# A one-core graph, scan and expert network: the lead-in of the scan stage, with the softplus of all channels ahead of step one

## The chip, the cores and the metric

The kernel runs on one core of one Trainium2 chip. A core has five instruction streams that run side by side and meet only at semaphores: TensorE (PE, matrix products into the PSUM memory), VectorE (DVE), ScalarE (ACT, functions of one tensor), GpSimd (POOL) and SyncE (SP, which here only issues transfers). Each stream takes its instructions strictly in order; an instruction that waits holds up everything behind it on the same engine. Transfers run on 16 DMA engines, whichever stream issued them. The metric is the device time of one execution in microseconds (us), lower is better.

## The reference

The input is `x` (4096 tokens of 256 features) and a sparse 4096 x 4096 matrix `adj`. Two layers follow each other, each a graph part and a mixture of experts. The change touches only the graph part of layer 0, a graph convolution with a Mamba block behind it:

```python
h = jax.nn.relu(adj @ x @ gcn_w + gcn_b)          # x already layer-normed
h = (h - mu) * lax.rsqrt(var + EPS) * ln_g + ln_b
xz = h @ w_in                                     # 256 -> 2 x 512 channels
xconv = sum(xpad[k:k + L] * conv_w[:, k] for k in range(4)) + conv_b
u = jax.nn.silu(xconv)
dbc = u @ w_xp                                    # 16 + 16 + 16 columns
dt = jax.nn.softplus(dbc[:, :16] @ w_dt + b_dt)   # 512 channels
dA = jnp.exp(dt[:, :, None] * A[None])            # 16 states per channel
dBu = dt[:, :, None] * B[:, None, :] * u[:, :, None]
hst = dAt * hst + dBut; y = hst @ Ct              # one token after the other
y = (y + u * D_skip) * jax.nn.silu(z) @ w_out
```

The scan over tokens is a recurrence for each of 512 x 16 pairs of channel and state. After it come the experts of layer 0 and the whole of layer 1, which the change leaves alone.

## The kernel before

**Chunks and steps.** The tokens are cut into 8 chunks of 512. For each chunk a *front* (class `Front`) prepares what the scan needs, and 32 *steps* (class `Step`) run the scan. The 512 channels are 4 blocks of 128 (`MB`), in two halves of two blocks (`H = 2`). A step covers 32 channels (a *group*, four to a block), four states on the partitions beside them and two states one after the other along the row, so 128 partitions by 1024 elements. A group is used in two steps: steps 0 to 3 are groups 0 to 3 with the first pair of states, steps 4 to 7 the same groups with the second pair.

**A step.** `inputs` (L1384, POOL) multiplies dt*u by B into `db`; `decays` (L1400, ACT, two instructions of 512) makes `da = exp(A*dt)`; `scan` (L1416, DVE) runs the recurrence over 1024 elements; `keep` (L1423, ACT) saves the last column in `state`; `product` (L1429, DVE) multiplies by C into `hc`, a ring of six buffers; `pair` (L1433) adds the two halves of `hc` by a transfer issued from POOL; `total` (L1441 and L1447, PE) sums groups into `psy`, two steps at a time and six steps late (`LAG = 6`); `gate` (L1455, DVE) finishes a block of channels.

**A front.** Its parts are methods named in two plans, `PLAN` and `EARLY`. In order: `do_gcn` (L949, PE), `do_biased` (L963, ACT), `do_stats` (L973, DVE), `do_normal` (L985, ACT), `do_turn` and `do_turned`, `do_xz` (L1016, PE), `do_conv` (L1033, PE), `do_silu` (L1043, ACT), `do_project` (L1053, PE), `do_scatter` (L1060, ACT, and a transfer to memory from which B and C are spread over partitions, L1126), `do_dt` (L1067, PE, one per block). Then softplus, written so that it keeps its accuracy, per half of the channels: `do_abs` takes the absolute value and the positive part (L1079, L1080, ACT, per block), `do_exp` (L1083, ACT) makes e = exp(-|v|), `do_plus` (L1086, L1087, ACT) makes (e + 1) - 1, `do_soft 0` (L1095, DVE) the rounding error of that, `do_log` (L1090, ACT) overwrites e with ln(1 + e), and `do_soft 1, 2, 3` (L1097, L1099, L1101, DVE) add up dt and make dt*u. `do_store` (L1108) writes both to memory, `dtd`, by two transfers from SP; `spread` (L1117) reads one group's 32 rows back from there with each row repeated on four partitions, into `dtu`, a ring of five buffers. ACT has a table of functions to load when it goes between exp, ln and silu; the loads are instructions of their own (ACT_TABLE_LOAD).

**The propagation** `adj @ x` of a later chunk (`propagation`, L877, PE) runs in *pieces* of two products among all this. A chunk has two halves of 32 pieces, 64 products. A product of 32-bit numbers is two passes on PE, and the rows of the profile count passes, so half a chunk is 128 of them. The adjacency comes in tiles `at` of 512 KB (L795, SP), three buffers, eight products to a tile. Both halves accumulate in one PSUM buffer `pt` (`ps_pt`, `bufs=1`); at the end of a half ACT copies it out into `pts` (L883), and the next half's first product waits for that copy. `advance(k)` emits k pieces, and where a half ends among them, the copy too.

**The order.** PE, DVE, ACT and POOL run in the order in which the program text emits instructions (a manual schedule); SP's order is set by a planner. The lead-in of chunk 0 runs the plans of its front with i from 4 to 26 and puts pieces of chunk 1's propagation behind single i by the table `FILL`:

```python
            prop, left = propagation(1), 2 * NT + 2 - late
            for i in range(4, 27):
                fr.at(i, Front.EARLY)
                fr.at(i)
                ...
                k = min(FILL.get(i, 0), left)
                advance(k)
                left -= k
            advance(left)
```

The first half of the channels passes softplus here (i = 20 to 25), its four groups are spread at i = 25, and the pieces that remain follow at i = 21, but for the last four, which fall into steps 0 to 2. The second half of the channels passes softplus inside steps 0 to 5 (L1596 puts i = 27 to 32 of front 0 into them). From step 3 on, the front of chunk 1 is worked on among the steps of chunk 0, and so on.

Of the kernel before, what the change touches and what calls it, by code (L numbers as in the profile page):

```python
# [10 lines left out]
F32 = mybir.dt.float32  # L11
BF16 = mybir.dt.bfloat16
I32 = mybir.dt.int32
AF = mybir.ActivationFunctionType
ALU = mybir.AluOpType
# [4 lines left out]
P = 128  # L20
CW = 512
# [25 lines left out]
def kernel(ctx: ExitStack, tc: tile.TileContext, out: bass.AP, **a):  # L47
    nc = tc.nc
# [6 lines left out]
    MB = DI // P  # L55
# [727 lines left out]
    with ExitStack() as s1:  # L783
        wp = s1.enter_context(tc.tile_pool(name="w_gnn0", bufs=1))
        w1p = s1.enter_context(tc.tile_pool(name="work1", bufs=1))
        w2p = s1.enter_context(tc.tile_pool(name="work2", bufs=2))
# [53 lines left out]
        H = MB // 2  # L840
        G4 = P // 32
# [4 lines left out]


        PE_RATIO = 1.0
        FILL = {6: 8, 7: 2, 9: 1, 12: 3, 14: 1, 17: 3, 18: 1, 19: 2, 20: 3, 21: 40}
        FILLED = {7: 1, 8: 2}  # L850
        PIECE, PE_STEP, DVE_STEP = 1.0, (1.8, 0.1), 4.25
        PE_COST = {"gcn": 2.5, "turn": 0.8, "xz": 2, "conv": 4, "project": 2, "dt": 1}
# [1 line left out]
        psts, fronts = {}, {}  # L854
# [44 lines left out]
        class Front:  # L899
# [24 lines left out]
            def __init__(self, c):  # L924
                self.c = c
                self.pts = psts.pop(c)
                self.dtd, self.dtu, self.bc = {}, {}, {}
                self.st = small.tile([P, TPC, 6], F32, name="ln_st")
                self.mv = small.tile([P, TPC, 2], F32, name="ln_mv")
                self.rs = small.tile([P, TPC], F32, name="ln_rs")  # L930
                self.nm = small.tile([P, TPC], F32, name="ln_nm")
                self.ps, self.psy = {}, {}
# [139 lines left out]
            def do_abs(self, m):  # L1072
                ps = self.ps.pop(("dt", m))
                b = m % H
                if b == 0:
                    self.sp = w1p.tile([P, 2, H, CW], F32, name="sp", tag="tmp")
                    self.t1 = w1p.tile([P, H, CW], F32, name="t1", tag="h")
                    self.dt, self.du = self.sp[:, 0], self.sp[:, 1]
                nc.scalar.activation(self.du[:, b, :], ps, AF.Abs, bias=b_dt[:, m:m + 1])  # L1079
                nc.scalar.activation(self.dt[:, b, :], ps, AF.Relu, bias=b_dt[:, m:m + 1])  # L1080

            def do_exp(self, a):
                nc.scalar.activation(self.du, self.du, AF.Exp, scale=-1.0)  # L1083

            def do_plus(self, a):
                nc.scalar.activation(self.t1, self.du, AF.Identity, bias=1.0)  # L1086
                nc.scalar.activation(self.t1, self.t1, AF.Identity, bias=minus1[:, :1])  # L1087

            def do_log(self, a):
                nc.scalar.activation(self.du, self.du, AF.Ln, bias=1.0)  # L1090

            def do_soft(self, a, i):
                t1, dt, du = self.t1, self.dt, self.du
                if i == 0:
                    nc.vector.tensor_tensor(t1, t1, du, ALU.subtract)  # L1095
                elif i == 1:
                    nc.vector.tensor_tensor(du, du, t1, ALU.subtract)  # L1097
                elif i == 2:
                    nc.vector.tensor_tensor(dt, dt, du, ALU.add)  # L1099
                else:  # L1100
                    nc.vector.tensor_tensor(  # L1101
                        du, dt, self.us[:, a * H:a * H + H, :], ALU.mult
                    )

            def do_store(self, a):
                self.dtd[a] = dram.tile([P, H, 2, CW], F32, name=f"dtd{self.c}_{a}")
                for k in range(2):
                    nc.sync.dma_start(self.dtd[a][:, :, k, :], self.sp[:, k])  # L1108
                fronts[self.c] = self

            def spread(self, g):

# [352 lines left out]
        with tc.manual_schedule(engines={  # L1465
# [13 lines left out]
            for _ in range(2 * NT + 2 - sum(FILLED.values())):  # L1479
                i = min(range(STEPS), key=lambda i: pe[i] - PE_RATIO * dve[i])  # L1480
# [4 lines left out]
            def advance(k=1, wait=False):  # L1485


                while k > 0:
                    k -= 1
                    if next(prop, None) and wait:  # L1490
                        break
                return k
# [50 lines left out]
            fr = Front(0)  # L1543
# [8 lines left out]
            for _ in range(EARLY_LISTS - NT // 4):  # L1552
                next(made)
            prop, left = propagation(1), 2 * NT + 2 - late
            for i in range(4, 27):
                fr.at(i, Front.EARLY)
                fr.at(i)
                if i == 6:
                    for _ in made:
                        pass  # L1560
                if i == 19:
                    for p in range(2):
                        fr.states("b", p)
                        fr.states("c", p)
                if i == 25:
                    for g in range(G4):
                        fr.spread(g)
                k = min(FILL.get(i, 0), left)
                advance(k)
                left -= k  # L1570
            advance(left)
            steps, tails, kept, gated, summed, owed = [], [], {}, [], 0, 0
            ALL = NC * STEPS
            for n in range(2):
# [4 lines left out]
            for n in range(ALL):  # L1579
                c, i = divmod(n, STEPS)  # L1580
                cur = steps[n]
                if i == 6 and c > 0:
                    if c < NC - 1:
                        kept[c - 1] = keep_gated(c - 1)
                    else:
                        tails.extend(Tail(c - 1, hh) for hh in range(2))
                if i == 8 and c == NC - 2:
                    tails.extend(
                        Tail(k, hh, kept[k], k < SLOW) for k in range(c) for hh in range(2)
                    )  # L1590
                if i == BEGIN:
                    fr = Front(c + 1) if c + 1 < NC else None
                    prop = propagation(c + 2) if c + 2 < NC else iter(())
                live = [(fronts[c], STEPS + i)] if n > 0 else []
                if c == 0 and i < 6:
                    live.insert(0, (fronts[0], 27 + i))  # L1596
                if i >= BEGIN and fr is not None:
                    live.append((fr, i))

                if n + 5 < ALL:  # L1600
                    c5, i5 = divmod(n + 5, STEPS)
                    if i5 % (2 * G4) < G4:
                        fronts[c5].spread(i5 // (2 * G4) * G4 + i5 % G4)
                if fr is not None:
                    if i == 27:
                        fr.states("b", 0)
                    elif i == 29:
                        fr.states("c", 0)
                    elif i == 30:
                        fr.states("b", 1)  # L1610
                if i == 1 and c > 0:
                    fronts[c].states("c", 1)

                cur.scan()
                cur.keep()
                if n + 1 < ALL:
                    steps[n + 1].join()
                if n + 2 < ALL:
                    steps.append(Step(n + 2))
                    steps[n + 2].decays()  # L1620
                for f, k in live:
                    f.at(k, Front.EARLY)
                if c == NC - 1 and i in NORMS:
                    NORMS[i]()
                if n > 0:
                    steps[n - 1].product()
                if n + 2 < ALL:
                    steps[n + 2].inputs()
                if n > 0:
                    steps[n - 1].pair()  # L1630
                for st in gated:
                    st.gate()
                gated = []
                if summed <= n - LAG or (summed <= n - 3 and not steps[summed].paired):
                    if steps[summed].total(steps[summed + 1]):
                        gated.append(steps[summed])
                    summed += 2
                for f, k in live:
                    f.at(k)
                for _ in range(TAILS.get((c, i), 1)):  # L1640
                    Tail.step(tails)
                if c == NC - 1:
                    for piece in NPIECES.get(i, ()):
                        piece()
                    if i == 24:
                        last = Last()
                        last.fetch()
                    elif i == 25:
                        last.first(0)
                    elif i == 27:  # L1650
                        last.residual(0)
                    elif i == 29:
                        for m in range(H, MB - 1):
                            last.add(0, m)
                owed = advance(pieces[i] + owed, True)
                if i == BEGIN - 1:
                    while owed:
                        owed = advance(owed, True)
# [613 lines left out]
```

## Time and profile before

| | us |
|---|---|
| median of 3 runs | 2342.67 |
| lowest and highest | 2336.9, 2344.26 |
| the profiled execution, its time | 2334.95 |
| its span, first to last instruction | 2333.1 |
| from the start to the first scan (L1416) | 171.94 |
| from the first scan to the start of the last | 1104.2 |
| from there to the end | 1057.0 |

The profiled execution lies 7.7 us under the median and 2.0 us under the lowest of the three runs; 1.85 us of its time lie outside the span. The profile is read by times from the start of the span. A row of the timeline gives the start, the duration, the engine, the line, the operation, what it writes and reads, the shape, how many instructions were merged (x), and in square brackets how long the engine stood idle before it and what ended that. PEld is the weight load of TensorE, SPq the time in which SP issues a transfer. The table by stretches gives each engine's busy time, TensorE's granted clock (1 is full), and the share of the DMA engines.

### The profile page before, as it was taken

Reading aid. Unit: us, or ns where it says so; the run is one execution under the profiler, and the core shown is the slowest. Engines: PE = TensorE matmul, PEld = TensorE weight load, DVE = VectorE, ACT = ScalarE, POOL = GpSimd, SP = SyncE. Lnnn points to the kernel's source line nnn. Section 1 sums busy time; section 2 is a strip of 40 time slices with the busy share of each in tenths; the row PEclk is TensorE's granted clock in tenths of the full one; section 3 lists DMA queues with packets and bytes.
Section 4 is the critical chain, followed back from the end, with each engine's and each line's share of the span. In section 5 each row is a group of like instructions: output and inputs, shape, how many; then the busy total and the mean of one; then the engine's idle time right before and its main releaser. Section 6 shows DMA issues by size and latency. Waiting matters only on the chain. (4 is left out here: it accounts for less than half of the span.)

```text
span 2333.1 us, 28789 instructions
## 1 busy us (share of the span) xinstructions
PE 2052.0 (88%) x8851; PEld 1451.2 (62%) x8851; DVE 1791.4 (77%) x2940; ACT 1308.2 (56%) x2386; POOL 1392.1 (60%) x1057
## 2 busy tenths in 40 slices
PE   7898989899998989988688699996899989899984
PEld 6665555555555564544355588784588778778773
DVE  4938999999999999998989699414438999954342
ACT  4136768677676867768686232322488778533221
POOL 1006777787777778776764354442057778856651
PEclk9899999999999999998788799998899999999997
DMA  7656897979889797887963799873355555477794
GB/s 240 212 168 177 203 286 170 273 180 247 220 199 281 168 273 183 241 226 193 259 190 122 228 346 354 280 225 114 118 178 173 179 160 180 142 237 221 251 307 150
DMA packets 299717, 498.77 MB, mean 214 GB/s; under 512 B 32459, under 2 KB 171711, under 8 KB 298656
## 3 DMA queue, kind: packets, MB, share of 16 engines
q1 hardware_dynamic: 241760, 383.28, 52.0%
q0 software_dynamic: 57792, 113.54, 21.5%
q8 instruction: 73, 1.20, 0.2%
q14 instruction: 92, 0.75, 0.1%
HBM read 384.01 MB, written 65.80 MB: 193 GB/s over the span
## 5 line engine op out<-in xcount | busy, mean ns | idle before, releaser
L1384 POOL TENSOR_TENSOR db<-dtu,bb 128x1024 f32<-128x1024 f32 x256 | 600.2, 2345 | 342.3 <-DVE hc L1429 177.4
L1416 DVE TENSOR_TENSOR_SCAN db<-da,state,db 128x1024 f32<-128x1024 f32 x256 | 599.1, 2340 | 44.5 <-ACT db L1409 29.8
L877 PE MATMUL pt<-at,gn 128*128 128x256 f32 x2048 | 487.7, 392 | 35.2 <-DMA at<-in_adjT_dram 18.1
L877 PEld LDWEIGHTS pt<-at,gn 128*128 128x128 f32 x2048 | 390.6, 195 | 144.2 <-issue 50.2
L1400 ACT ACTIVATE da<-dtu,negA 128x512 f32<-128x512 f32 (+1 forms) x512 | 350.2, 684 | 26.5 <-DMA dtu<-dtd 14.3
L1429 DVE TENSOR_TENSOR hc<-db,cb 128x1024 f32<-128x1024 f32 x256 | 341.5, 1334 | 15.3 <-PE psy L1447 15.2
L1962 PE MATMUL pf<-gn,f 128*128 128x256 f32 x1280 | 288.7, 386 | 0.0
L1962 PEld LDWEIGHTS pf<-gn,f 128*128 128x128 f32 x1280 | 246.9, 194 | 37.0 <-issue 3.3
L712 PE MATMUL ps_h<-xkT,wk 128*128 128x256 f32 x864 | 214.8, 390 | 15.8 <-DVE xkT L737 11.7
L697 PE MATMUL ps_y<-wk,hk 128*128 128x256 f32 x864 | 213.1, 382 | 0.2
L702 DVE TENSOR_TENSOR yk<-ps_y,bk 128x512 f32<-128x512 f32 x73 | 50.1, 686 | 205.7 <-PE ps_y L697 175.6
L1433 POOL DMA_DIRECT2D hc<-hc x232 | 201.8, 870 | 0.2
L712 PEld LDWEIGHTS ps_h<-xkT,wk 128*128 128x128 f32 x864 | 159.1, 193 | 54.2 <-DVE xkT L737 19.0
L1824 POOL DMA_INDIRECT x<-gnd,ls_idx x128 | 149.3, 1166 | 60.7 <-DMA gnd<-gn 21.3
L697 PEld LDWEIGHTS ps_y<-wk,hk 128*128 128x128 f32 x864 | 161.8, 191 | 21.9 <-ACT hk L716 1.4
L1423 ACT COPY state<-db 128x2 f32<-128x2 f32 x224 | 42.9, 191 | 218.5 <-DVE db L1416 218.3
L1016 PE MATMUL ps_xz<-hT,w_in 128*128 128x512 f32 x256 | 133.0, 669 | 33.1 <-ACT zs L1029 20.1
L1447 PE MATMUL psy<-hc,pick 128*32 128x256 f32 x1120 | 158.5, 411 | 0.0
L1824 POOL DMA_INDIRECT ring<-gnd,ls_idx x88 | 110.3, 1253 | 31.3 <-issue 11.9
L716 ACT ACTIVATE hk<-ps_h,d0r_b 128x256 f32<-128x256 f32 x104 | 49.1, 474 | 137.5 <-PE ps_h L712 132.3
L1447 PEld LDWEIGHTS psy<-hc,pick 128*32 128x32 f32 x1120 | 57.4, 116 | 106.7 <-issue 79.1
L1033 PE MATMUL ps_xz<-xc,dK 128*128 128x512 f32 x256 | 115.2, 598 | 0.0
(422 smaller groups left out, 3228.5 us busy)
## 6 DMA issues: line engine op xcount, KB each, us to landing
at<-in_adjT_dram SPq DMA_DIRECT2D x208, 512.0 KB, 4.4
dtu<-dtd SPq DMA_DIRECT2D x128, 512.0 KB, 5.8
hc<-hc POOLq DMA_DIRECT2D x232, 256.0 KB, 5.6
wk<-in_L_ffn_W_dram SPq DMA_DIRECT2D x70, 512.0 KB, 6.0
wk<-in_L_ffn_expert_w_dram SPq DMA_DIRECT2D x114, 256.0 KB, 4.0
dtd<-sp SPq DMA_DIRECT2D x32, 512.0 KB, 5.5
ls_at<-in_adj_dram SPq DMA_DIRECT2D x32, 512.0 KB, 8.0
hc<-in_adj_dram SPq DMA_DIRECT2D x16, 512.0 KB, 6.5
```

Of the source, the lines that this page charges most:

```text
L697: nc.tensor.matmul(ps[:, j, :], hT[:, m, j * P:(j + 1) * P], w[:, m, :], start=(m == 0), stop=(m == kb_out - 1),)
L712: nc.tensor.matmul(ps[:, j, :], w[:, d, m * P:(m + 1) * P], xT[:, d, :], start=(d == 0), stop=(d == DB - 1),)
L877: nc.tensor.matmul(pt[:, k, :], xl[:, j, k * P:(k + 1) * P], at[:, jj, :], start=(j == 0 and k == 0), stop=(j == NT - 1 and k == DB - 1),)
L1016: nc.tensor.matmul(ps, w_in[:, k, m * P:(m + 1) * P], self.hT[:, k, :], start=(k == 0), stop=(k == DB - 1),)
L1384: nc.gpsimd.tensor_tensor(self.db, self.dtu[:, 1:2, :].to_broadcast([P, 2, CW]), self.f.bc["b", self.p], ALU.mult,)
L1400: nc.scalar.activation(da[self.n % 2][:, j, j:], self.dtu[:, 0, j:], AF.Exp, scale=negA[:, q, m, s_:s_ + 1],)
L1416: nc.vector.tensor_tensor_scan(flat, da[self.n % 2].rearrange("p a t -> p (a t)"), flat, state[:, self.g, 2 * self.p:2 * self.p + 1], ALU. ...
L1429: nc.vector.tensor_tensor(self.hc, self.db, self.f.bc["c", self.p], ALU.mult)
L1433: nc.gpsimd.dma_start(self.hc[:, 0, :], self.hc[:, 1, :], accum_op=ALU.add)
L1447: nc.tensor.matmul(f.psy[r, t], pick, st.hc[:, j, t], start=False, stop=(self.p == 1 and j == last and w == 1),)
L1824: nc.gpsimd.indirect_dma_start(out=to[:, :], out_offset=None, in_=gnd[:, :], in_offset=bass.IndirectOffsetOnAxis(ap=lists.idx[:, q, s:s + ...
L1962: nc.tensor.matmul(pf[:, t, :], f[:, jj, t * P:(t + 1) * P], gn[:, j, :], start=(j == 0 and t % 2 == 0), stop=(j == NT - 1 and t % 2 == 1),)
```

## The change

In chunk 0 the softplus of all four blocks now stands in the lead-in, ahead of step 0, written out as calls in place of the plan. The second half of the channels gets `hc` buffers of its own for its three tensors. For chunk 0 `do_plus` is one DVE instruction in place of two on ACT. The first four groups' rows are no longer read back from memory: `straight` copies them on chip, from the 32 partitions of `dt` (k = 0) or dt*u (k = 1) to 128 partitions, by eight transfers issued from ACT's stream. The stores of chunk 0 to `dtd` (four transfers, used by the later groups) are issued from ACT as well, no longer from SP. Five pieces of the propagation stand ahead of `do_dt` of blocks 2 and 3 (two from i = 19, three by `FILL[20]`), and the others come after the second store, the last four in steps 0 to 2 as before. Steps 0 to 5 lose the calls for front 0's second softplus. What other chunks do is not changed.

```diff
-        FILL = {6: 8, 7: 2, 9: 1, 12: 3, 14: 1, 17: 3, 18: 1, 19: 2, 20: 3, 21: 40}
+        FILL = {6: 8, 7: 2, 9: 1, 12: 3, 14: 1, 17: 3, 18: 1, 19: 2, 20: 3}
...
             def do_abs(self, m):
                 ps = self.ps.pop(("dt", m))
                 b = m % H
-                if b == 0:
+                a = m // H
+                if b == 0 and self.c == 0 and a == 1:
+                    self.dt[a], self.du[a], self.t1[a] = (
+                        w2p.tile([P, 2, CW], F32, name="hc", bufs=6) for _ in range(3)
+                    )
+                elif b == 0:
                     self.sp = w1p.tile([P, 2, H, CW], F32, name="sp", tag="tmp")
...
             def do_plus(self, a):
-                nc.scalar.activation(self.t1, self.du, AF.Identity, bias=1.0)
-                nc.scalar.activation(self.t1, self.t1, AF.Identity, bias=minus1[:, :1])
+                t1, du = self.t1[a], self.du[a]
+                if self.c == 0:
+                    nc.vector.tensor_scalar(t1, du, 1.0, -1.0, ALU.add, ALU.add)
+                    return
+                nc.scalar.activation(t1, du, AF.Identity, bias=1.0)
+                nc.scalar.activation(t1, t1, AF.Identity, bias=minus1[:, :1])
...
             def do_store(self, a):
                 self.dtd[a] = dram.tile([P, H, 2, CW], F32, name=f"dtd{self.c}_{a}")
-                for k in range(2):
-                    nc.sync.dma_start(self.dtd[a][:, :, k, :], self.sp[:, k])
+                for k, t in enumerate((self.dt[a], self.du[a])):
+                    (nc.sync if self.c else nc.scalar).dma_start(self.dtd[a][:, :, k, :], t)
                 fronts[self.c] = self
+
+            def straight(self, k):
+
+                for g in range(G4):
+                    if k == 0:
+                        self.dtu[g] = w2p.tile([P, 2, CW], F32, name="dtu", bufs=5)
+                    rows = self.sp[32 * g:32 * g + 32, k, 0, :]
+                    nc.scalar.dma_start(
+                        self.dtu[g][:, k, :],
+                        bass.AP(rows.tensor, rows.offset, [rows.ap[0], (0, G4), *rows.ap[1:]]),
+                    )
...
-            for i in range(4, 27):
+            for i in range(4, 20):
...
-                if i == 25:
-                    for g in range(G4):
-                        fr.spread(g)
                 k = min(FILL.get(i, 0), left)
                 advance(k)
                 left -= k
-            advance(left)
+            for m in range(H):
+                fr.do_abs(m)
+            fr.do_exp(0)
+            fr.do_plus(0)
+            fr.do_soft(0, 0)
+            advance(FILL[20])
+            for m in range(H, MB):
+                fr.do_dt(m)
+            fr.do_abs(H)
+            fr.do_log(0)
+            for m in range(H + 1, MB):
+                fr.do_abs(m)
+            fr.do_exp(1)
+            for i in range(1, 4):
+                fr.do_soft(0, i)
+            for k in range(2):
+                fr.straight(k)
+            fr.do_store(0)
+            fr.do_plus(1)
+            fr.do_soft(1, 0)
+            fr.do_log(1)
+            for i in range(1, 4):
+                fr.do_soft(1, i)
+            fr.do_store(1)
+            advance(left - FILL[20])
...
-                if c == 0 and i < 6:
-                    live.insert(0, (fronts[0], 27 + i))
```

More of the change, by code (lines that the diff above doesn't have):

```diff
@@ L927, in __init__ @@
                 self.dtd, self.dtu, self.bc = {}, {}, {}
+                self.dt, self.du, self.t1 = {}, {}, {}
                 self.st = small.tile([P, TPC, 6], F32, name="ln_st")
@@ L1074, in do_abs @@
                 b = m % H
-                if b == 0:
+                a = m // H
[4 more added lines that the diff above has]
+                elif b == 0:
                     self.sp = w1p.tile([P, 2, H, CW], F32, name="sp", tag="tmp")
[L1077 to L1080, printed above, removed]
+                    self.t1[a] = w1p.tile([P, H, CW], F32, name="t1", tag="h")
+                    self.dt[a], self.du[a] = self.sp[:, 0], self.sp[:, 1]
+                nc.scalar.activation(self.du[a][:, b, :], ps, AF.Abs, bias=b_dt[:, m:m + 1])
+                nc.scalar.activation(self.dt[a][:, b, :], ps, AF.Relu, bias=b_dt[:, m:m + 1])
             def do_exp(self, a):
-                nc.scalar.activation(self.du, self.du, AF.Exp, scale=-1.0)
+                nc.scalar.activation(self.du[a], self.du[a], AF.Exp, scale=-1.0)
             def do_plus(self, a):
-                nc.scalar.activation(self.t1, self.du, AF.Identity, bias=1.0)
-                nc.scalar.activation(self.t1, self.t1, AF.Identity, bias=minus1[:, :1])
+                t1, du = self.t1[a], self.du[a]
[4 more added lines that the diff above has]
+                nc.scalar.activation(t1, t1, AF.Identity, bias=minus1[:, :1])
             def do_log(self, a):
-                nc.scalar.activation(self.du, self.du, AF.Ln, bias=1.0)
+                nc.scalar.activation(self.du[a], self.du[a], AF.Ln, bias=1.0)
             def do_soft(self, a, i):
-                t1, dt, du = self.t1, self.dt, self.du
+                t1, dt, du = self.t1[a], self.dt[a], self.du[a]
                 if i == 0:
```

## The prediction

> **What bounds the kernel now.** I read the table by stretches first, then the timeline of all engines over the lead-in, then VectorE's and TensorE's own timelines over the first steps. Row by row, the stretches are the lead-in, the first nine steps, the other steps, and all that follows the scan.
>
> ```profile
> 0.00:172.00 172.00, 145.83 (x558) 110.28 (x559) 102.54 (x321) 49.71 (x90) 13.34 (x26) 0.94 0.63 204
> 172.00:214.00 42.00, 34.71 (x115) 20.80 (x115) 34.98 (x30) 26.70 (x46) 26.21 (x16) 0.88 0.72 204
> 214.00:1276.00 1062.00, 948.53 (x3892) 569.88 (x3890) 995.91 (x666) 765.40 (x1567) 784.98 (x483) 0.94 0.83 218
> ```
>
> The third number after the length is VectorE: 995.91 of 1062 us (94%) from step 8 on, but 34.98 of 42 (83%) before. So a shift of VectorE at step 8 reaches the end of the kernel undiminished, and what can be gained lies ahead of 214. The lead-in, all engines:
>
> ```profile
> 143.50 8.90 PE L877 MATMUL pt<-at,gn 128*128 128x256 f32 x40
> ...
> 146.48 1.06 ACT L1083 ACTIVATE sp<-sp 128x1024 f32<-128x1024 f32 x1
> ...
> 152.43 0.59 ACT L883 COPY pts<-pt 128x512 f32<-128x512 f32 x1 [2.63 <-PE pt L877]
> 153.04 1.28 ACT L1090 ACT_TABLE_LOAD   x1
> ...
> 154.25 24.55 PE L877 MATMUL pt<-at,gn 128*128 128x256 f32 x112 [1.86 <-DMA at<-in_adjT_dram]
> ...
> 155.42 1.23 DVE L1097 TENSOR_TENSOR sp<-sp,t 128x1024 f32<-128x1024 f32 x1 [4.35 <-ACT sp L1090]
> ...
> 157.98 0.55 SPq L1108 DMA_DIRECT2D dtd<-sp  x1
> ...
> 171.94 2.35 DVE L1416 TENSOR_TENSOR_SCAN db<-da,state,db 128x1024 f32<-128x1024 f32 x1 [12.77 <-POOL db L1384]
> ...
> 186.73 0.57 ACT L883 COPY pts<-pt 128x512 f32<-128x512 f32 x1
> ...
> 186.85 1.22 DVE L1095 TENSOR_TENSOR t<-t,sp 128x1024 f32<-128x1024 f32 x1 [6.19 <-ACT t L1087]
> ```
>
> Two things are to be seen. VectorE waits 12.77 us for step 0 and 6.19 us in step 2, where the second softplus stands; that is the prize. And the two copies L883 sit tight behind PE: at 152.43 ACT waits for PE, and PE goes on at 154.25, delayed by a transfer alone. VectorE's steps (scans 4, 6, 8, and two products that waited for PE), then TensorE:
>
> ```profile
> 193.85 2.34 DVE L1416 TENSOR_TENSOR_SCAN db<-da,state,db 128x1024 f32<-128x1024 f32 x1
> ...
> 205.59 2.34 DVE L1416 TENSOR_TENSOR_SCAN db<-da,state,db 128x1024 f32<-128x1024 f32 x1
> ...
> 213.47 2.34 DVE L1416 TENSOR_TENSOR_SCAN db<-da,state,db 128x1024 f32<-128x1024 f32 x1
> ...
> 227.99 1.23 DVE L1429 TENSOR_TENSOR hc<-db,cb 128x1024 f32<-128x1024 f32 x1 [1.48 <-PE psy L1447]
> ...
> 236.05 1.23 DVE L1429 TENSOR_TENSOR hc<-db,cb 128x1024 f32<-128x1024 f32 x1 [0.99 <-PE psy L1447]
> ```
>
> ```profile
> 198.30 6.34 PE L1016 MATMUL ps_xz<-hT,w_in 128*128 128x512 f32 x8 [5.46 <-ACT h L963]
> ...
> 210.04 5.40 PE L1016 MATMUL ps_xz<-hT,w_in 128*128 128x512 f32 x8 [1.83 <-ACT zs L1029]
> ...
> 220.79 3.60 PE L1016 MATMUL ps_xz<-hT,w_in 128*128 128x512 f32 x8
> ```
>
> The same eight passes take 3.60 us in a busy stretch, 6.34 after 5.46 us idle, 5.40 after 1.83: a PE that stood still restarts at about half speed and loses 1.8 to 2.7 us.
>
> **The change part by part.** The built program of the changed kernel gives the order on each engine; times are from the rows.
>
> *Gone from the steps:* four VectorE sums (1.22 to 1.40 us), on ACT four absolute values and positive parts, the exp, two additions, the ln and a table load, and the 6.19 us that VectorE waited. *Gone from SP:* four stores and four reads at about 0.55 us each; nothing waits for SP's time here, so that saves nothing.
>
> *Softplus in one piece.* ACT is as before up to the end of the first exp, 147.54. PE does ten products more (20 passes x 8.90/40 = 4.45 us, to 147.95), then the two products for blocks 2 and 3 (1.98, to 149.9), then the ten that end the first half: 154.4, where it was 152.4. On ACT: absolute value and positive part of block 2 at 149.1 (as before, 1.16 us after their product began) to 150.35; table load and ln to 152.7; block 3 to 154.0; table load and exp to 156.4. The addition moved to VectorE is not shown in this form; the bounds are 0.77 (an L870 row, half the output bytes) and 1.23 us (L1097). I take 1.23; either ends, with `do_soft 0`, by 150.0, before ACT gets to the ln, so it costs nothing; if ACT came sooner, up to 1.2. VectorE's sums follow the ln at 1.26 apart: dt at 155.3, dt*u at 156.5.
>
> *Ten transfers in ACT's stream* (eight copies, two stores) stand from 155.3 between ACT and the second ln. ACT issues none in the trace of before. Low bound: nothing for issuing, but the built program makes the eighth copy wait for the first to land and the stores for the second copy and for an adjacency tile asked for at 154.4; with 4.4 us for a tile (median of the `at` loads) the second ln starts at 159 to 159.5. High bound: 0.87 us each, as POOL issues (L1433), to 164. I take SP's pitch in the B and C reads (142.88, 143.46, 144.10, 144.74: 0.6 each), the nearest row as it issues the same kind: 155.3 + 6.0 = 161.4. Then table load and ln 2.35, three sums 3.75, the second store 0.6, the copy L883 0.6: **the first copy ends at 168.7** (166.5 to 171.5). It stood at 153.0.
>
> *The wait that this adds.* The second half of the propagation needs that copy, since there is one `pt`. PE, with nothing else in its order, stands from 154.4 to 168.7. Behind it: 128 passes x 24.55/112 = 28.1 us, plus 2.5 for the restart (between the two rows above): 199.3. *On ACT*, the second copy stands behind the decays of step 3 and ahead of those of step 4; ACT waits there with everything queued behind until 199.9. It ended at 187.3 before. The SP queue's read of group 4 waits for the first store and holds back the adjacency loads behind it to about 167, but their buffers are only free at 172, so that is hidden by PE's stall (without it: up to 6 us).
>
> *Step 0* is not earlier either: its decays follow the first copy and a table load of 1.3: scan at 171.4 against 171.94. Its rows, copied by about 163, and POOL's 2.35 us are hidden; the on-chip copying gains 0.5.
>
> *Steps 4 to 8.* Decays of step 4 end at 201.5, scan at 201.6 against 193.85: +7.7. VectorE idles from about 185. Then the missing softplus pays: 3.6 us to scan 5 (4.70 before), 5.8 to scan 6 (7.04), the same 7.9 to scan 8: 218.9 against 213.47, **+5.4**.
>
> *PE catches up a little.* From 199.3: the graph products 6.6, eight passes 1.75, the z products warm 3.5 where 6.2 followed idling, eight passes 1.75: the first total starts at 213.0 (206.21). The next z products wait for ACT until 215.6 (210.04) after a shorter idle; warm, they end 3.8 later than before, cold 5.4. VectorE's two waits for PE (1.48, 0.99) shrink accordingly, so the shift that remains lies between 3.8 and 5.4: **+4.6 us**. Against the profiled execution's own 2334.95 that is 2339.6; on the median of the runs, 2342.67, it is **2347**. Each us of the first copy is a us of the result: break-even at 164.1.
>
> [...]
>
> **The rivals.** *Faster: the copies do not hold PE.* If PE's second half ran as early as now, scans would run from 171.4 at 3.57 us a step with 2.3 for the statistics of chunk 1: scan 8 at 202.3 in place of 213.47, 11 us gained, 2331. The idle 6.19 speaks for it; against it, the copy comes in ACT's order behind a store that needs the last sum. It decides if the first copy ends by 157.
>
> *Slower: transfers cost ACT more than SP.* At 0.87 to 1.1 us each (the first L1433 rows: 0.87 to 1.13), the first copy ends at 171.4 to 173.9, the sum is +7.3 to +9.8; landings as slow as those of `dtu` (5.8) add up to 1: 2350 to 2354. It decides from 0.84 us per transfer (first copy at 171.1). The wide, repeated read from 32 partitions, which no row shows, speaks for it; SP's even 0.6 speaks against.
>
> *Nothing to measure: cheap issue.* At the low bound the copy ends at 166.5 and the sum is +2.4; with PE's clock at 1.0 instead of 0.88 between 172 and 214 after its rest, another 3 us go: 2342.
>
> **How the numbers follow.** Differences under 0.3% (7.0 us) can't be told from no change here: the three runs spread over 7.4. Forecast 0.40, cheap issue 0.12, dear issue 0.33, faster 0.15. The forecast's own spread (first copy by 2 us, restart by 1, the measurement by 3) leaves a quarter of it above +7, the rest within; the cheap case is within, the dear one all but 0.03 above, the faster one all but 0.02 below. Slower 0.40, same 0.47, faster 0.13. The range drops the faster case and the outermost of the dear one: 2336 to 2356; the forecast alone is 2342 to 2352.
>
> **What would show it.** Right: PE idle some 14 us before L877's second half, released by ACT's copy; the second copy near 200; scan 0 within 1 us of 172; scan 4 near 201; scan 8 near 219; no more 6.19. Wrong: ACT spending well under or over 6 us on the ten transfers, first copy outside 166 to 172, or VectorE's rhythm after step 8 other than now.

## The result, and the profile after

The changed kernel takes 2345.95 us (median of 20 runs, 2338.96 to 2350.98) beside 2338.34 us for the kernel before (20 runs, 2328.79 to 2344.26). The ratio is 1.0035, with a 95% interval of 1.0021 to 1.0048: slower, by 7.6 us between the medians. Its profiled execution is the slowest of the 20, with a time of 2350.98 us and a span of 2349.1. One execution of a run below (transfers from SP) took 2484.97 us at a granted clock of 0.81; it is left out of that run's time and ratio.

The stretches of the profile after, cut as before (lead-in, first nine steps, other steps); columns are busy time of PE, PEld, DVE, ACT, POOL, then PE's clock, the DMA share and GB/s:

```profile
0.00:172.00 172.00, 129.49 (x480) 94.99 (x480) 107.06 (x324) 51.34 (x92) 17.92 (x28) 0.90 0.63 200
172.00:214.00 42.00, 37.55 (x153) 30.53 (x154) 20.49 (x13) 12.90 (x24) 10.69 (x7) 0.87 0.57 167
214.00:1276.00 1062.00, 948.27 (x3881) 568.73 (x3881) 998.78 (x675) 767.45 (x1571) 791.30 (x489) 0.94 0.84 219
```

From 214 on VectorE is as busy as it was (998.78 against 995.91). The loss is in the two rows above: PE does 16 us less in the lead-in, and VectorE 14 us less in the first steps. ScalarE's timeline says why (ACTq is the time in which ACT's sequencer issues transfers):

```profile
154.78 1.06 ACT L1089 ACTIVATE hc<-hc 128x1024 f32<-128x1024 f32 x1
154.86 9.20 ACTq L1127 DMA_DIRECT2D dtu<-sp  x8
164.10 3.39 ACTq L1118 DMA_DIRECT2D dtd<-sp  x2
167.57 1.28 ACT L1100 ACT_TABLE_LOAD   x1 [11.74 <-DMA dtu<-sp]
168.87 1.06 ACT L1100 ACTIVATE hc<-hc 128x1024 f32<-128x1024 f32 x1
173.99 1.78 ACTq L1118 DMA_DIRECT2D dtd<-hc  x2
175.81 0.58 ACT L883 COPY pts<-pt 128x512 f32<-128x512 f32 x1 [5.88 <-DVE hc L1111]
...
207.40 0.58 ACT L883 COPY pts<-pt 128x512 f32<-128x512 f32 x1 [22.04 <-PE pt L877]
```

Eight copies and two stores hold ACT's stream for 12.7 us (154.86 to 167.57). Their rows stand end to end, so ACT waits for nothing between them. The second ln is behind them, the sums behind the ln, the second pair of stores behind the sums, and the copy L883 behind all that. VectorE and TensorE:

```profile
169.96 2.74 DVE L1107 TENSOR_TENSOR hc<-hc 128x1024 f32<-128x1024 f32 x1 [12.01 <-ACT hc L1100]
172.73 1.23 DVE L1109 TENSOR_TENSOR hc<-hc 128x1024 f32<-128x1024 f32 x1
173.99 1.23 DVE L1111 TENSOR_TENSOR hc<-hc,us 128x1024 f32<-128x1024 f32 x1
179.23 4.59 DVE L1437 TENSOR_TENSOR_SCAN db<-da,state,db 128x1024 f32<-128x1024 f32 x2 [4.01 <-ACT da L1421]
...
209.50 2.35 DVE L1437 TENSOR_TENSOR_SCAN db<-da,state,db 128x1024 f32<-128x1024 f32 x1 [17.43 <-ACT state L1444]
...
226.49 2.34 DVE L1437 TENSOR_TENSOR_SCAN db<-da,state,db 128x1024 f32<-128x1024 f32 x1
...
247.44 1.22 DVE L1450 TENSOR_TENSOR hc<-db,cb 128x1024 f32<-128x1024 f32 x1 [0.74 <-PE psy L1468]
```

```profile
149.43 4.58 PE L877 MATMUL pt<-at,gn 128*128 128x256 f32 x20
176.45 30.92 PE L877 MATMUL pt<-at,gn 128*128 128x256 f32 x128 [22.44 <-ACT pts L883]
...
215.67 3.60 PE L1017 MATMUL ps_xz<-hT,w_in 128*128 128x512 f32 x8
...
223.05 3.70 PE L1017 MATMUL ps_xz<-hT,w_in 128*128 128x512 f32 x8 [0.21 <-ACT zs L1030]
```

PE stands for 22.44 us until ACT's copy, and then does the whole second half in one piece. VectorE's waits of 12.77 us ahead of step 0 and 6.19 for the second softplus are gone; in their place stand 12.01 us ahead of the second sums, 4.01 ahead of step 0 and 17.43 ahead of step 4, and scan 8 starts at 226.49, 13.0 us later. The z products (L1017) now run almost without a gap in 3.60 and 3.70 us, where they took 6.34 and 5.40. One line of the page's table of groups sums it up for the whole kernel: the propagation's largest wait is now for that copy, 28.8 us, where it was 18.1 us for the adjacency's tiles. Before, then after:

```profile
L877 PE MATMUL pt<-at,gn 128*128 128x256 f32 x2048 | 487.7, 392 | 35.2 <-DMA at<-in_adjT_dram 18.1
L877 PE MATMUL pt<-at,gn 128*128 128x256 f32 x2048 | 492.4, 395 | 49.8 <-ACT pts L883 28.8
```

### The profile page after: what moved, and what is told of

The parts are those of the page before. It is cut to its first block, busy times and chain, and to the rows that moved or that the text cites. A ratio compares the mean times of both kernels' runs of the same rounds, so it can differ in the third digit from the quotient of the medians.

```text
span 2349.1 us, 28799 instructions
## 1 busy us (share of the span) xinstructions
PE 2053.9 (87%) x8851; PEld 1456.0 (62%) x8851; DVE 1793.6 (76%) x2942; ACT 1303.8 (56%) x2382; POOL 1392.9 (59%) x1057
## 5 line engine op out<-in xcount | busy, mean ns | idle before, releaser
L877 PE MATMUL pt<-at,gn 128*128 128x256 f32 x2048 | 492.4, 395 | 49.8 <-ACT pts L883 28.8
L1421 ACT ACTIVATE da<-dtu,negA 128x512 f32<-128x512 f32 (+1 forms) x512 | 350.0, 684 | 12.1 <-DVE db L1437 3.6
L1017 PE MATMUL ps_xz<-hT,w_in 128*128 128x512 f32 x256 | 129.3, 653 | 26.7 <-ACT zs L1030 18.1
L1864 POOL DMA_INDIRECT ring<-gnd,ls_idx x88 | 110.3, 1253 | 31.3 <-DVE x L1880 12.7
```

Of the source, the lines that this page charges most:

```text
L877: nc.tensor.matmul(pt[:, k, :], xl[:, j, k * P:(k + 1) * P], at[:, jj, :], start=(j == 0 and k == 0), stop=(j == NT - 1 and k == DB - 1),)
L1017: nc.tensor.matmul(ps, w_in[:, k, m * P:(m + 1) * P], self.hT[:, k, :], start=(k == 0), stop=(k == DB - 1),)
L1421: nc.scalar.activation(da[self.n % 2][:, j, j:], self.dtu[:, 0, j:], AF.Exp, scale=negA[:, q, m, s_:s_ + 1],)
L1864: nc.gpsimd.indirect_dma_start(out=to[:, :], out_offset=None, in_=gnd[:, :], in_offset=bass.IndirectOffsetOnAxis(ap=lists.idx[:, q, s:s + ...
```

## The experiments

**The theory.** The copy L883 is late because it stands in ACT's order behind ten transfers, the second softplus and two stores; PE waits for it, and step 4 waits for PE. **Its rivals:** the softplus of all channels ahead of step 0 costs time by itself; the on-chip copies hold something else up; or ACT is simply a slow issuer. The first runs move one thing each; the last two also move the copy and some pieces of the propagation. Times in the table are from their profiles, in us. A ratio is to the kernel before as measured beside that run: 2338.34 us for the first result, 2336.24 (29 runs) for the changed kernel again, the copy early and the transfers from SP, 2338.83 (23 runs) for the last three. The "marker" is the start of the first scan behind the scan stage (L295), so it tells what reaches the end of the stage; from it to the end of the span the runs take 1048 to 1055 us, but for the one marked in the last column.

| run | first copy ends | scan 0 | second copy ends | scan 4 | scan 8 | marker | ratio (95%) |
|---|---|---|---|---|---|---|---|
| before | 153.0 | 171.9 | 187.3 | 193.9 | 213.5 | 1284.7 | |
| before, again | 151.8 | 171.8 | 188.5 | 195.1 | 214.7 | 1285.5 | |
| after | 176.4 | 179.2 | 208.0 | 209.5 | 226.5 | 1294.2 | 1.0035 (1.0021 to 1.0048) |
| after, again | 175.9 | 178.8 | 205.9 | 207.4 | 224.4 | 1294.1 | 1.0042 (1.0026 to 1.0059) |
| copy early | 156.1 | 177.9 | 190.4 | 191.9 | 208.9 | 1282.9 | 0.9979 (0.9963 to 0.9996) |
| transfers from SP | 160.3 | 165.9 | 197.9 | 199.4 | 216.4 | 1286.6 | 1.0008 (0.9991 to 1.0024) |
| plain rows | 171.4 | 174.2 | 202.4 | 203.9 | 220.9 | 1290.0 | 1.0197 (1.0173 to 1.0220), marked |
| copies from POOL | 155.1 | 172.3 | 193.3 | 194.8 | 211.8 | 1285.6 | 0.9985 (0.9971 to 1.0000) |
| rows from memory | 155.9 | 168.9 | 190.0 | 191.5 | 208.5 | 1280.0 | 0.9965 (0.9951 to 0.9980) |

### The two kernels again

No edit to either; the changed kernel and the kernel before, each profiled a second time.

> The changed kernel once more, to see how far its lead-in moves from one execution to the next. Theory: what sets the loss is the end of the first copy out of the accumulator (176.4 us in the first profile), because the product engine waits for it; if so it ends within 2 us of 176.4 again, TensorE stands idle 20 to 24 us ahead of the second half, scan 8 starts within 2 us of 226.5, and the ratio to the kernel before is 1.003 to 1.005. Rival (the copy's place was an accident of one execution, and the loss lies elsewhere): the copy ends below 172 and the ratio stays above 1.003.

> The kernel before once more, for its profile. If executions differ in the stages behind the scan and not in the scan, the first scan starts within 1 us of 171.9, scan 8 within 1 us of 213.5, the last scan within 3 us of 1276.1, and what differs in the span lies behind it.

The changed kernel took 2344.76 us, ratio 1.0042; the kernel before, in one execution, 2335.58. ACT's ten transfers take 12.1 us (12.7 the first time), PE's wait is 22.11 us, the marker is 8.6 us behind that of the kernel before (9.6 in the first pair). In the first profile after, the part behind the marker was 6.5 us longer than before (1054.9 against 1048.4); here both have 1048.3. So those 6.5 us belong to that execution and not to the change. Scan 8 came 2.1 us earlier than in the first profile of the changed kernel, and 1.2 us later than in the first of the kernel before: each just outside what was expected.

### The copy early

Five pieces that end the first half, and its copy L883, are emitted right behind the second exp, ahead of the transfers. Nothing else moves in the program text.

```diff
             fr.do_exp(1)
+            advance(6)
             for i in range(1, 4):
                 fr.do_soft(0, i)
...
-            advance(left - FILL[20])
+            advance(left - FILL[20] - 6)
```

> Only the first copy moves: the last five pieces of the half and the copy are emitted behind the second exp, ahead of the ten transfers of ACT. Theory (the copy's place in ACT's order is the loss): TensorE is idle under 3 us ahead of the second half, the second copy ends at 184 to 187, scan 0 stays at 177 to 180 because the second ln still stands behind the transfers, scan 4 at 190 to 194, scan 8 at 208 to 211 against 213.5 before and 226.5 changed; ratio to before 0.997 to 1.000. Rival (the transfers' traffic, or the bunched softplus itself, costs the time): scan 8 at 215 or later and a ratio of 1.002 or more.

It took 2330.89 us: faster than both kernels (2336.24 for the kernel before beside it). ACT's order, then PE's:

```profile
154.60 1.30 ACTq L1127 DMA_DIRECT2D dtu<-sp  x2
155.49 0.57 ACT L883 COPY pts<-pt 128x512 f32<-128x512 f32 x1
155.94 8.31 ACTq L1127 DMA_DIRECT2D dtu<-sp  x6
164.29 2.88 ACTq L1118 DMA_DIRECT2D dtd<-sp  x2
167.25 1.28 ACT L1100 ACT_TABLE_LOAD   x1 [11.20 <-DMA dtu<-sp]
...
189.78 0.59 ACT L883 COPY pts<-pt 128x512 f32<-128x512 f32 x1 [5.78 <-PE pt L877]
```

```profile
156.10 16.01 PE L877 MATMUL pt<-at,gn 128*128 128x256 f32 x64 [2.35 <-ACT pts L883]
173.04 7.17 PE L877 MATMUL pt<-at,gn 128*128 128x256 f32 x32 [0.92 <-DMA at<-in_adjT_dram]
182.57 7.17 PE L877 MATMUL pt<-at,gn 128*128 128x256 f32 x32 [2.36 <-DMA at<-in_adjT_dram]
```

The transfers are as dear as ever and the second ln starts at 167.25, as late as in the changed kernel; scan 0 stays at 177.9. Yet the whole loss is gone, and 1.8 to 2.6 us at the marker more than that, because PE waits 2.35 us and not 22.44. So the long transfers cause the loss through the copy that stands behind them; scan 0, which they make 6 us later than before, does not set step 4. That the early softplus or the transfers' traffic is the loss is ruled out. The second copy ends 3 us later than expected (190.4), since PE still waits 0.92 and 2.36 us for tiles.

### All transfers from SP

The eight copies and the four stores go to SP's stream; the order on ACT stays otherwise.

```diff
-                    (nc.sync if self.c else nc.scalar).dma_start(self.dtd[a][:, :, k, :], t)
+                    nc.sync.dma_start(self.dtd[a][:, :, k, :], t)
...
-                    nc.scalar.dma_start(
+                    nc.sync.dma_start(
                         self.dtu[g][:, k, :],
```

> Only the issuer changes: all twelve transfers of chunk 0's lead-in go from ACT's stream to SP's; the copy stays behind the second store in the program. Theory: ACT is then held by VectorE's sums alone, the second ln ends near 159 to 160, the first copy at 162 to 166, TensorE is idle 8 to 12 us, the second copy ends at 193 to 197, scan 8 at 212 to 217; ratio 0.999 to 1.002. If ACT's own issuing is slow, SP's twelve rows are all 0.5 to 0.7 us; if it is the backlog of the DMA engines, SP too has rows of 2 us among the copies. Rival (the copy's place does not matter): ratio as the changed kernel's, 1.003 or more.

It took 2338.31 us, no difference from the kernel before (2336.24). The second ln's table load starts at 157.45 and the first copy ends at 160.3, earlier than the 162 to 166 expected, so ACT is free; PE waits 6.89 us for the copy, less than the 8 to 12 expected. But SP needs as long for the same transfers as ACT did. SP's timeline, and PE's:

```profile
154.32 8.84 SPq L1127 DMA_DIRECT2D dtu<-sp  x8
163.25 2.34 SPq L1118 DMA_DIRECT2D dtd<-sp  x2
165.71 2.62 SPq L1118 DMA_DIRECT2D dtd<-hc  x2
168.41 3.26 SPq L795 DMA_DIRECT2D at<-in_adjT_dram  x3
```

```profile
160.33 9.14 PE L877 MATMUL pt<-at,gn 128*128 128x256 f32 x32 [6.89 <-ACT pts L883]
174.69 22.60 PE L877 MATMUL pt<-at,gn 128*128 128x256 f32 x96 [5.22 <-DMA at<-in_adjT_dram]
```

ACT is no slow issuer: 8.84 us on SP, 9.20 on ACT. The queue moves the loss instead of removing it: the adjacency's tiles now stand behind the transfers on SP, and PE waits 5.22 us for one. So the second copy ends at 197.9, just past the 193 to 197 expected.

### Plain rows

The eight copies read all 128 partitions once, in place of the 32 partitions of a group with every row repeated (four times; the expectation's "sixteen" is a slip). Bytes written and number of transfers stay. The first four groups of chunk 0 so get wrong rows of dt and dt*u; the expectation's "second chunk" is a slip too.

```diff
-                    rows = self.sp[32 * g:32 * g + 32, k, 0, :]
+                    rows = self.sp[:, k, 0, :]
...
-                        bass.AP(rows.tensor, rows.offset, [rows.ap[0], (0, G4), *rows.ap[1:]]),
+                        rows,
```

> Part changed: the eight straight copies read 128 partitions once instead of each group's rows repeated sixteen times, so the first four groups of the second chunk get the wrong rows of dt*u; bytes written and number of transfers stay. If the repeated read from few partitions makes the long rows (copies of about 2 us among copies of 0.6), the eight copies take about 5 us instead of 9.2, the second ln starts near 162 instead of 167.6, the first copy ends near 170 and the ratio falls to about 1.001. If the backlog of the queues makes them (the adjacency's tiles in flight and the copies' own bytes), the rows, the second ln (166 to 168), the first copy (175 to 176) and the ratio (1.004) stay.

The lead-in answers the question. ACT's timeline:

```profile
153.67 5.75 ACTq L1127 DMA_DIRECT2D dtu<-sp  x8
159.46 1.36 ACTq L1118 DMA_DIRECT2D dtd<-sp  x2
160.91 1.28 ACT L1100 ACT_TABLE_LOAD   x1 [6.26 <-DMA dtu<-sp]
```

The ten transfers take 7.2 us where they took 12.7. Of the three sums behind the second ln, two now run beside POOL's products (2.38 and 3.25 us, then 1.23 alone; 6.9 in all), so the first copy ends at 171.4 and not at 170. The instructions of L1127 one by one (minimum, median and maximum in ns), first of the changed kernel and then of this run:

```profile
L1127 ACTq DMA_DIRECT2D dtu<-sp x8: 561/857/2273, 154.9 to 163.3; - x8
...
DMA to landing us min/median/max: 4.9/4.9/5.6
```

```profile
L1127 ACTq DMA_DIRECT2D dtu<-sp x8: 533/627/869, 153.7 to 158.7; - x8
...
DMA to landing us min/median/max: 3.7/3.7/3.8
```

And the stretch of the copies, in the changed kernel and in this run:

```profile
156.20:164.00 7.80, 0.00 (x0) 0.00 (x0) 1.72 (x2) 0.00 (x0) 0.00 (x0) 0.66 0.90 238
```

```profile
154.50:159.50 5.00, 0.00 (x0) 0.00 (x0) 2.23 (x3) 0.14 (x1) 0.00 (x0) 0.65 1.03 381
```

The DMA engines are taken up in both (share 0.90 and 1.03), but the stretch with the repeated read moves 238 GB/s and the one with the plain read 381, the adjacency's tiles in flight included. So it is the way the rows are read, and not the number or the bytes of the transfers, that makes single issues up to 2.27 us long there and 0.87 at most here; how a slow read holds its issuer was not shown. The run changes two things at once, the number of partitions read (32 to 128) and the repetition of rows (every row four times, or once); which of them counts, no run here separates. The expectation that the rows would stay long whatever is read is disproved.

The time of the whole run, 2384.7 us, where a ratio of 1.001 was expected, must not be read as a price: the marker is 4.3 us earlier than in the changed kernel, and all that is lost lies behind it (1087.3 us in place of 1054.9). The wrong rows change what reaches the experts, and with it the amount of work; the weight loads of one line of the experts, after and here:

```profile
L712 PEld LDWEIGHTS ps_h<-xkT,wk x864: 185/190/365, 1327.3 to 2312.8; 128*128 128x128 f32 x173
```

```profile
L712 PEld LDWEIGHTS ps_h<-xkT,wk x928: 185/190/338, 1323.0 to 2341.2; 128*128 128x128 f32 x186
```

### Copies from POOL

The copy early (with one piece of the second half), the eight on-chip copies issued by POOL, the four stores by SP, emitted behind the softplus (SP, whose order is planned, still starts the first pair at 153.7); eight more pieces stand behind the last sum.

```diff
-                    (nc.sync if self.c else nc.scalar).dma_start(self.dtd[a][:, :, k, :], t)
+                    nc.sync.dma_start(self.dtd[a][:, :, k, :], t)
...
-                    nc.scalar.dma_start(
+                    nc.gpsimd.dma_start(
...
             fr.do_exp(1)
+            advance(7)
...
-            fr.do_store(0)
...
+            advance(8)
+            fr.do_store(0)
             fr.do_store(1)
-            advance(left - FILL[20])
+            advance(left - FILL[20] - 15)
```

> Straight copies issued by GpSimd, both stores by SyncE behind the softplus, the propagation's first copy on ScalarE ahead of the second ln. If ScalarE's order is the whole loss: the second ln near 157.5, the first copy ends near 155.5, scan 0 near 166, second copy 186 to 188, scan 4 near 188, scan 8 near 205 and a ratio of 0.996 to 0.998. Rival, the straight copies hold GpSimd or land late and scan 0 stays near 172 to 178: then scan 4 near 192, scan 8 near 209, ratio 0.998 to 1.000.

It took 2335.47 us, at the edge of what can be told from the kernel before (0.9971 to 1.0000). The first copy ends at 155.1 as expected, but scan 0 starts at 172.3, as the rival had it. POOL's timeline, then a row of PE's:

```profile
154.31 4.60 POOL L1127 DMA_DIRECT2D dtu<-sp  x8 [54.43 <-DVE sp L1109]
169.89 6.95 POOL L1405 TENSOR_TENSOR db<-dtu,bb 128x1024 f32<-128x1024 f32 x3 [10.98 <-DMA dtu<-sp]
```

```profile
173.68 19.01 PE L877 MATMUL pt<-at,gn 128*128 128x256 f32 x80 [6.19 <-DMA at<-in_adjT_dram]
```

POOL issues at an even 0.58 us each, but its own first product, which needs the fifth of the copies, waits for it until 169.89; it started at 164.68 in the changed kernel and at 163.56 with the transfers from SP. What the issuer doesn't wait for here, the reader does (10.98 us). Why the rows come later was not tried; SP issued two stores and two of the adjacency's tiles in the same stretch (153.70 to 160.61). Scan 0 is not what sets the time here, though: PE stands 6.19 us for a tile, the second copy ends at 193.3 in place of the 186 to 188 expected, and steps 4 and 8 follow it, some 3 us later than even the rival had them.

### Rows from memory

As the last run, but without the on-chip copies: the first four groups are read back from memory, as in the kernel before, behind the first pair of stores.

```diff
             fr.do_exp(1)
+            advance(7)
...
-            for k in range(2):
-                fr.straight(k)
             fr.do_store(0)
+            for g in range(G4):
+                fr.spread(g)
...
+            advance(8)
             fr.do_store(1)
-            advance(left - FILL[20])
+            advance(left - FILL[20] - 15)
```

> Softplus of all channels first and the propagation's first copy early, as in the last run, but the straight copies are undone: the first four groups' rows come from memory, behind the first store. If the straight copies are worth little once ScalarE does not issue them: scan 0 at 170 to 172, second copy near 186, scan 4 at 188 to 191, scan 8 near 206, ratio 0.997 to 0.999. If the straight copies carry the gain of the last run: scan 0 at 175 or later, scan 8 at 210 or later, and a ratio of 0.999 to 1.001.

It took 2331.65 us beside 2338.83, ratio 0.9965, just past the 0.997 to 0.999 expected. Scan 0 starts at 168.9, earlier than with the copies from POOL (172.3) and than the expectation for either theory. SP issues the four reads from memory in 2.72 us from 161.80, ACT's first decays wait for the first rows until 166.46, and what sets step 4 (191.5) is again the second copy, 4 us later than the 186 expected, after a wait of PE of 3.62 us for a tile:

```profile
166.46 2.75 ACT L1421 ACTIVATE da<-dtu,negA 128x512 f32<-128x512 f32 x4 [5.22 <-DMA dtu<-dtd]
...
189.42 0.58 ACT L883 COPY pts<-pt 128x512 f32<-128x512 f32 x1 [14.33 <-PE pt L877]
```

So the on-chip copies bring no time that these runs show: issued from SP they gave the earliest scan 0 of all (165.9), but step 4 waits for the second copy. The place of the pieces and the copy behind the transfers costs what is lost; and what remains in this run to explain its gain is, as far as these runs tell, the softplus ahead of step 0, without the 6.19 us wait in step 2 (scan 8 at 208.5 for 214.7, the marker 5.5 us earlier than in the second profile of before). That part alone, with the pieces where they were, was not run. This run and the copy early can't be told apart (0.9951 to 0.9980 and 0.9963 to 0.9996); both are faster than both kernels.

## Why the prediction was right or wrong

**The time came out for a mixed reason.** 2347 was said and 2345.95 measured, but the shift was +7.6 us and not +4.6, and the kernel before has a median of 2338.34 over 20 runs, 4.3 under that of the three runs that the shift was added to. The two errors nearly cancel, so the closeness of the number is luck. The forecast's mechanism, and that it makes the kernel slower, was right; a size was off. By its own chances a difference too small to tell (0.47) was likelier than a slower kernel (0.40), and +4.6 was among the differences that it took for too small to tell. Of its signs of being right, the end of the 6.19 us wait and PE's wait for ACT's copy came; scan 0, scan 4, scan 8 and the second copy all came 7 to 8.5 us later than it said.

**The added wait** was right in kind and place: PE stands ahead of the second half until ACT's copy, ACT stands ahead of the second copy, step 4 is late. It was said to be 14 us and is 22.4. One reading behind it was off without effect: before, only the first copy sits tight behind PE. The second half ended at 184.37 (180.65 and 3.72 us) and ACT came to its copy at 186.73, behind the second softplus.

**Ten transfers in ACT's stream** is the term that was mis-sized. At SP's pitch of 0.6 us each it was 6.0 us, with the second ln at 161.4; measured, 12.7 us and 167.6, beyond even the high bound of 164, and over 6 us spent there was one of its signs of error. SP's even pitch came from four reads from memory; it did not carry over to copies that read 32 partitions with every row repeated, on ACT or on SP. The run with plain rows has 7.2 us and 160.9.

**The rival "transfers cost ACT more than SP"** is the case that came, by the prediction's own mark (0.84 us per transfer; they took 1.27, beyond the rival's upper end of 1.1). Its shift of +7.3 to +9.8 is right, its 2350 to 2354 is not, for the same reason as above; and its name is wrong, as SP takes as long as ACT. Its argument, the repeated read from 32 partitions, is what the plain rows bear out: the eight issue rows took 9.20 us and 5.75, the copies landed 4.9 and 3.7 us after their issue (medians), and the stretches moved 238 and 381 GB/s with all that was in flight. Whether it is the number of partitions or the repetition of the rows, no run here shows.

**The three sums behind the second ln** were put at 3.75 us and took 5.3: the first took 2.74 us in place of 1.23, while POOL ran its products (164.68 to 171.61). With the late ln (+6.2) and these 1.5, the first copy ended at 176.4 in place of 168.7; outside 166 to 172 was another of the signs of error.

**Step 0** was said to hold at 171.4 and started at 179.2, 7.8 us later, nearly all of it these 7.7, since its decays follow the first copy. **Steps 4 to 8** were right: 17.3 us from scan 4 to scan 8 by the prediction, 17.0 measured. **The restart** of PE was put at 2.5 us over 28.1; the 128 passes took 30.92 us after and 29.28 when run again, so 1.2 to 2.8. In the first profile the granted clock stood at 0.50 for the first 6.15 us of them (176.45 to 182.60), and at 1.00 behind that; if nothing but the clock differs, the 1.64 us between the two rows make some 2.9 us at 0.50 in the second, an estimate. So the loss is no single number. The ln starts 1.30 us behind the start of its table load (167.57, 168.87), as the prediction took it.

**PE catches up** was too small. Shift at scan 8: +13.0, at the marker +9.6 (first pair), and +9.7 and +8.6 (second pair). 1.1 to 3.4 us are absorbed behind step 8, not the 0.8 that was taken. One part of it can be named: from scan 10 to scan 14 the shift of the first pair falls from 13.0 to 11.4 us, as VectorE's two waits for PE's sums there before (1.48 and 0.99) are gone; waits of that kind come later instead (0.74 at 247.44, 1.51 at 277.86). The shift is 12.2 at scan 224 and 9.6 at the last, and nothing here explains that fall. So the prediction's first reading, that a shift at step 8 reaches the end undiminished, does not hold to the microsecond. The rule "each us of the first copy is a us of the result" would have given +12.3; it counts too much.

**The softplus in one piece** cost nothing on the path, as said. Its addition on VectorE took 0.69 us, under the low bound of 0.77, without effect.

**The rival "the copies do not hold PE"** put a first copy by 157 at 2331 us. The copy early made it so (156.1) and took 2330.89. The agreement in time is partly luck: scan 8 was said to be at 202.3 and is at 208.9, as scan 0 stayed late and PE still waits for tiles; and here too the kernel before is faster than the one that 2331 was reckoned from. **"Cheap issue"** did not occur.

## What to carry to other kernels

When transfers are put into the stream of an engine that computes, price them from rows of transfers that read in the same way, not by the pitch of another kind, and look first at how many partitions they read and whether rows are repeated (here eight copies took 9.20 us to issue from 32 partitions with every row repeated, 5.75 from 128 read once). Then ask which instruction behind them frees a single buffer: here one copy of 0.58 us, moved ahead of the transfers, turned +7.6 us into a gain of 5.4. Moving the transfers to another engine moved the wait here to what stands behind them there (5.22 us of PE for a tile behind SP's), or to the reader (POOL's first product, 5.2 us later).

## What the runs showed of the hardware that was not expected

- Single issues among eight equal copies took 0.56 to 2.27 us on ACT (first profile of the changed kernel) and 0.56 to 1.99 us on SP; POOL issued the same eight at 0.55 to 0.77 us, and its first product got its rows 5.2 us later than in the changed kernel (169.89 for 164.68).
- A stretch of copies that read 32 partitions with each row repeated ran at 238 GB/s with the DMA engines 90% taken; one with the same number of bytes per copy, read from 128 partitions, ran at 381.
- The first of VectorE's sums of 128x1024 behind the second ln (with plain rows the second too) took 2.31 to 3.25 us beside POOL's products (the changed kernel twice, the copy early, the plain rows); these sums took 1.22 to 1.23 with no product on POOL (the runs with transfers from SP, with copies from POOL and with rows from memory).
- After standing for 22.44 us TensorE's granted clock stayed at 0.50 for the first 6.15 us of work in one execution of the changed kernel, where 128 passes took 30.92 us; in another, after 22.11 us, they took 29.28.
